# First layer of a two-layer kernel: steps that begin with a quarter of the tokens, a bit-search router, rows moved by indirect DMA

## The chip, the cores and the metric

The kernel runs on one core of a Trainium2 chip. The metric is the device time of one execution in microseconds. The core's engines each run their own instruction stream in order: TensorE (PE; its weight loads are shown as PEld), VectorE (DVE), ScalarE (ACT), GpSimd (POOL) and SyncE (SP), which issues most of the DMAs.

## What is computed

Two layers over one sequence of 2048 tokens of width 128. Each layer computes `x = x + s * silu(f)` from `xn = layernorm(x)`. In the first layer `s` is an attention with relu in place of softmax, 16 heads of width 8, and `f` is a routed transformer block over few tokens. The second layer (causal softmax attention, 16 heads of width 64, and a gated feed-forward) isn't touched by the change.

```python
# first layer, s: relu attention over all 2048 tokens
q, k, v = split((xn @ w_qkv).reshape(B, S, 16, 24))
w = relu(q @ k.T / sqrt(8))
out = (w / (sum(w) + 1e-6)) @ v
s = layernorm(xn + out @ w_out + b_out) * gamma + beta
# first layer, f: the routed block
weights = xn @ router_w + router_b
topv, topi = top_k(weights, 256)
thr = topv[-1]
sel_mask = weights > thr
sel_idx = sort(topi[:255])
x_sel, pos_sel, w_sel = xn[sel_idx], pos[sel_idx], weights[sel_idx]
...   # rmsnorm, 16-head softmax attention with rope, rmsnorm, gelu feed-forward
proc = x2 * w_sel
f = zeros_like(xn).at[sel_idx].set(proc) + xn * (1 - sel_mask)
```

## The kernel before

**Steps.** `relu_attention` runs the first layer as 256 steps. Step n belongs to a query chunk of 512 tokens (n // 64), a group of four heads (n // 16 % 4) and a block of 128 keys (n % 16). `scores(n)` makes four matmuls at once in four row strips of the array (L824), each 32 rows deep, and four relus of 512 columns (L832 on ScalarE, L834 on VectorE). `products(n)` comes two steps later and multiplies the relus by the values (L840). The scores have six PSUM banks, all other work has one bank called `x`.

**High and low parts.** Queries and keys are given to TensorE as a rounded high part and a low rest, so that a group of four heads fills 128 rows: per head 4 combinations of 8 values. For head group 0 a projection makes that layout directly (`project`, L703, L708, L709). For the other groups `spread` (L728 to L738) projects 512 tokens for all heads, makes both parts and writes them by four DMAs of 256 KB into a DRAM tile; `group` (L742) reads one head group of it back, 256 KB, into `kT` or a query tile.

**Before the steps.** `begin` normalises all four blocks of 512 tokens (`normalised`, L774 to L785, then four transposes L101 and a copy L103 into `xnT`), projects the keys of all four blocks for head group 0, the queries of block 0, and the values of all 16 key blocks (`values`, L756, L760). Then step 0 begins.

**Who else works among the steps.** TensorE, ScalarE and VectorE take their instructions in the order of the program. GpSimd and SyncE do not: the framework's planner orders theirs, by what it finds ready. After each step either one piece of `due` is done (a projection with its spread) or the generator `others()` goes on by one turn, that is, to the next `yield`. The generator is the routed block, then the loading of second-layer weights, then the closing of each query chunk (`gated`), which waits until its chunk is `ready`. `work` keeps two running sums, of ScalarE and VectorE microseconds as the author put them down, and `work.lesser` gives each relu to the engine with the lesser sum. These lines set the places:

```python
    due = {1: (all_queries, 0)}
    read = {}
    for i in range(NQ):
        due[4 + 4 * i] = (all_keys, i)
        for g in range(1, G):
            read[8 + 4 * i if g == 1 else 16 * g - 10 + 3 * i] = (g, i)
    for qc in range(1, NQ):
        due[64 * qc - 24] = (all_queries, qc)
```

**The routed block** (`routed_block`). Its set-up (loads, iotas and memsets) precedes its first `yield`, which is taken before `begin`. It makes the router weights of all tokens as a row on every partition (`wrow`, L281, L282) and turns them into columns of 128 (`wcol`, L289, L290). For each of 16 columns it counts on VectorE how many tokens stand ahead of each of the column's 128 tokens (L303, L310, L314): the token's rank, ties by position. From the ranks it makes one-hot matrices (L331) and gathers the selected 256 rows, with weight, index and position, by matmul (L341, sums in L346); a further matmul (L353) takes the threshold. A mask gather by indirect DMA, two normalisations, attention, feed-forward and `proc` (L626) follow. The result is put in place by one-hot matmuls over all tokens (one-hots L642, matmuls L652), added to the unselected rows (L658), and gated (L667 to L674).

In turns: the router rows and columns take steps 0 to 10, the counts 11 to 36, the gather 37 to 46, the block 47 to 127, the placing 128 to 139. From 224 to 255 the generator has nothing to do but wait for the last chunk.

Of the kernel before, what the change touches and what calls it, by code (L numbers as in the profile page):

```python
# [35 lines left out]
NS = 6  # L36
NEG = -1.0e30
# [68 lines left out]
def layer0(ctx, tc, a, small, ident, xin, xn1T, row_load, second):  # L106
# [17 lines left out]
    w_k = keep.tile([P, 4, 4, HD0], F32, name="w_k")  # L124
    w_q = keep.tile([P, 4, 4, HD0], F32, name="w_q")
    for i in range(4):
        for t, dst in ((1, w_k), (0, w_q)):
            nc.gpsimd.tensor_copy(dst[:, :, i, :], w_qkv[:, 0, :, t, :])
# [9 lines left out]
    for n, bit in (("k", 16), ("q", 8)):  # L138
        b = small.tile([P, 1], I32, tag="low_bit")
        nc.vector.tensor_scalar(b, prow, bit, None, ALU.bitwise_and)  # L140
        f = keep.tile([P, 1], F32, name=f"low_{n}")
        nc.vector.tensor_copy(f, b)
        nc.vector.tensor_scalar(f, f, -1.0 / bit, None, ALU.mult)
        lows.append(f)
# [72 lines left out]
def routed_block(  # L217
# [12 lines left out]
    for t, n in enumerate(("wq", "wk", "wv")):  # L230
# [11 lines left out]


    tok = rb.tile([P, 512], F32, name="tok")
    nc.gpsimd.iota(
        tok, pattern=[[1, 512]], base=0, channel_multiplier=0,
        allow_small_or_imprecise_dtypes=True,
    )
    before = rb.tile([P, P], F32, name="before")
    nc.gpsimd.memset(before, 1.0)  # L250
    nc.gpsimd.affine_select(
        out=before, in_=before, pattern=[[-1, P]], compare_op=ALU.is_gt,
        fill=0.0, base=0, channel_multiplier=1,
    )
    last = rb.tile([P, P], F32, name="last")
    nc.gpsimd.memset(last, 1.0)
    nc.gpsimd.affine_select(
        out=last, in_=last, pattern=[[0, P]], compare_op=ALU.is_ge,
        fill=0.0, base=-(P - 1), channel_multiplier=1,
    )  # L260
    nc.gpsimd.iota(
# [5 lines left out]
    qk = rb.tile([P, 2 * H, 32], F32, tag="qk_p4", name="qk")  # L267
    nc.gpsimd.memset(qk, 0.0)
    v = rb.tile([P, 2, H, 32], F32, name="r_v")
# [3 lines left out]
    yield  # L273
# [20 lines left out]


    junk = rb.tile([P, S], BF16, tag="junk_mrows", name="junk")
    cnt = rb.tile([P, 3, NC], F32, name="cnt")
    nc.vector.memset(cnt, 0.0)
    for c in range(NC):
        w = wcol[:, c : c + 1]  # L300
        lo = c * P
        if c:
            nc.vector.tensor_scalar(  # L303
                junk[:, :lo], wrow[:, :lo], w, None, ALU.is_ge, ALU.add,
                accum_out=cnt[:, 0, c : c + 1],
            )
            if c >= NC // 2:
                work.add(d=0.2 + lo / 960)
                yield
        nc.vector.tensor_scalar(  # L310
            junk[:, lo:], wrow[:, lo:], w, None, ALU.is_gt, ALU.add,
            accum_out=cnt[:, 1, c : c + 1],
        )
        nc.vector.scalar_tensor_tensor(  # L314
            junk[:, :P], wrow[:, lo : lo + P], w, before, ALU.is_equal, ALU.mult,
            accum_out=cnt[:, 2, c : c + 1],
        )
        work.add(d=2.9 if c < NC // 2 else 2.7 - lo / 960)
        yield
    rank = rb.tile([P, NC], F32, name="rank")  # L320
    nc.vector.tensor_reduce(rank, cnt.rearrange("p a c -> p c a"), AX.X, ALU.add)
# [3 lines left out]
    made = []  # L325
    for c in range(-2, NC, 2):
        hots = made
        if c + 2 < NC:
            made = [rw.tile([P, KSEL], F32, tag="og", bufs=4, name="hot") for _ in range(2)]
            for i in range(2):  # L330
                nc.vector.tensor_scalar(  # L331
                    made[i], tok[:, :KSEL], rank[:, c + 2 + i : c + 3 + i], None, ALU.is_equal
                )
            work.add(d=0.7)
        if c < 0:
            yield
            continue
        t = bank([P, 2, 131])
        for b in range(2):
            for i in range(2):  # L340
                nc.tensor.matmul(  # L341
                    t[:, b, :], hots[i][:, b * P : (b + 1) * P], xne[:, c + i, 0:131],
                    start=(i == 0), stop=(i == 1),
                )
        if c:
            nc.vector.tensor_tensor(xs, xs, t, ALU.add)  # L346
        else:
            nc.vector.tensor_copy(xs, t)
        work.add(d=0.5)
        yield  # L350
    thr = small.tile([P, 1], F32, tag="thr")
    t = bank([P, 1])
    nc.tensor.matmul(t, last, xs[:, 1, 128:129], start=True, stop=True)  # L353
    nc.vector.tensor_copy(thr, t)
# [278 lines left out]
    at = small.tile([P, 2, NQ], F32, tag="at")  # L633
    for i in range(NQ):
        nc.gpsimd.tensor_scalar(at[:, :, i], xs[:, :, 129], 512.0 * i, None, ALU.subtract)
    for i in range(NQ + 1):
        if i:
            put = place
        if i < NQ:
            place = [rw.tile([P, 512], F32, tag="prT", bufs=4, name=f"place{b}") for b in range(2)]  # L640
            for b in range(2):
                nc.vector.tensor_scalar(place[b], tok, at[:, b, i : i + 1], None, ALU.is_equal)  # L642
            work.add(d=1.0)
            yield
        if not i:
            continue
        cs = slice(4 * i - 4, 4 * i)
        t = bank([P, 4, D])
        for c4 in range(4):
            for b in range(2):  # L650
                n = KB[b]
                nc.tensor.matmul(  # L652
                    t[:, c4, :], put[b][:n, c4 * P : (c4 + 1) * P], proc[:n, b, :],
                    start=(b == 0), stop=(b == 1),
                )
# [21 lines left out]
        yield  # L677


def relu_attention(  # L680
# [19 lines left out]
    def project(dst, w, i, low, tag="x"):  # L700

        t = bank([P, 512], tag)
        nc.tensor.matmul(  # L703
            t, w.rearrange("p b a d -> p (b a d)"), xnT[:, 512 * i : 512 * i + 512],
            start=True, stop=True,
        )
        high = aw.tile([P, 512], F32R, tag="high", name="high")
        nc.scalar.copy(high, t)  # L708
        nc.vector.scalar_tensor_tensor(dst, high, low, t, ALU.mult, ALU.add)  # L709
        work.add(a=0.6, d=0.75)  # L710

    def keys(i):
        project(kT[:, 0, 512 * i : 512 * i + 512], w_k, i, low_k, "s")
# [7 lines left out]
    def queries():  # L721
        project(query_tile(0, 0), w_q, 0, low_q, "s")

    def spread(w, i, order):

# [8 lines left out]
        nc.vector.scalar_tensor_tensor(parts[1], parts[0], -1.0, t, ALU.mult, ALU.add)  # L734
        work.add(a=0.6, d=0.75)
        rows = dram.tile([G, 4, 4, HD0, 512], F32, tag="spread", bufs=8, name="spread")
        for n, x in enumerate(order):
            nc.sync.dma_start(out=rows[:, :, n, :, :], in_=parts[x].bitcast(F32))  # L738
        return rows

    def group(rows, g, dst):
        nc.sync.dma_start(out=dst.bitcast(F32), in_=rows[g].rearrange("j n d q -> (j n d) q"))  # L742

    asked, key_rows = {}, {}

    def all_keys(i):
        key_rows[i] = spread(w_ka, i, (0, 0, 1, 1))

    def all_queries(qc):
        asked[qc] = spread(w_qa, qc, (0, 1, 0, 1))  # L750
# [43 lines left out]

    def begin():
        parts = [normalised(i) for i in range(NQ)]
        next(parts[0])
        for i in range(NQ):
            if i + 1 < NQ:
                next(parts[i + 1])  # L800
# [925 lines left out]
```

## Time and profile before

| | us |
|---|---|
| median of 3 runs | 1487.89 (1487.07 to 1488.57) |
| the profiled execution | 1487.12 |
| its span, first to last instruction | 1485.1 |
| first scores of step 0 | 37.7 |
| first scores of step 12 | 63.1 |
| first scores of step 38 | 115.4 |
| first scores of step 128 | 296.9 |
| end of the 256 steps | about 503 |

In the profile "busy" is the time in which an engine had an instruction at work. Lines such as L824 are lines of the kernel as printed above. A stretch names the busy microseconds of each engine with the number of instructions in brackets, then the mean granted TensorE clock (1.00 is full), the share of the DMA engines that was busy, and GB/s. A row of the timeline has its start, its length, engine, line, operation, output and inputs, shape and count; neighbours of one kind are merged. A float32 matmul shows as two records. SPq marks the issue of a DMA by SyncE, not the transfer.

### The profile page before, as it was taken

To read this page: it belongs to the slowest core of one execution; us is meant where nothing else is said; L and a number is where in the kernel's file an instruction comes from. 1 tells how busy PE (TensorE), PEld (TensorE's weight loads), DVE (VectorE), ACT (ScalarE), POOL (GpSimd) and SP (SyncE) were. 2 spreads that over 40 slices of the span, in tenths; PEclk is the share of its full clock that TensorE was granted. 3 is DMA by queue.
4 is the path that set the end of the run, shared out by engine and by line. 5 is a ranking of instruction groups with operands and counts; after the bars stand their busy time and mean duration, and the time that the engine had idled before them with its cause. 6 is when DMAs were issued, how large, how long until landed. Compare 5 with 4: busy or idle time off the path is not lost.

```text
span 1485.1 us, 27124 instructions
## 1 busy us (share of the span) xinstructions
PE 1431.8 (96%) x10336; PEld 877.3 (59%) x10336; DVE 1079.6 (73%) x1938; ACT 967.2 (65%) x2080; POOL 325.2 (22%) x445
## 2 busy tenths in 40 slices
PE   4999999999999999999999999999999999999997
PEld 2223233332222367777777777777777777777775
DVE  5797878778888667567677667667767766777765
ACT  2787878778878656656556556556656655665663
POOL 1001000050000123322332242242242232252310
PEclk8999999999999999999999999999999999999999
DMA  2621100100200220000010010010001001000000
GB/s 66 186 66 61 32 12 14 49 26 14 60 20 4 79 50 15 15 16 15 21 24 15 15 30 15 15 29 15 15 15 29 15 15 29 15 15 16 15 22 22
DMA packets 28192, 44.70 MB, mean 30 GB/s; under 512 B 5984, under 2 KB 14560, under 8 KB 28064
## 3 DMA queue, kind: packets, MB, share of 16 engines
q1 hardware_dynamic: 27376, 41.94, 11.0%
q8 instruction: 81, 1.33, 0.4%
q0 software_dynamic: 256, 0.79, 0.2%
q14 instruction: 47, 0.39, 0.1%
q10 hardware_dynamic: 432, 0.26, 0.1%
HBM read 14.76 MB, written 10.11 MB: 17 GB/s over the span
## 4 chain that ended last, share of the span: by engine, by line
PE 60%; ACT 2%; DVE 1%; issue 1%; DVEq 0%; ACTq 0%
PE t L1326 18%; PE z L1376 17%; PE t L1556 16%; PE m L1436 2%; PE m L1264 2%; PE m L1229 2%; PE m L1279 2%; PE m L1421 2%; ACT p L1360 1%; ACT pt L1563 1%; PE m L1158 0%; DVE tops L1347 0%; PE m L1176 0%; DVE t L1346 0%; DVE pt L1563 0%
## 5 line engine op out<-in xcount | busy, mean ns | idle before, releaser
L1347 DVE TENSOR_REDUCE tops<-t 128x1 f32<-128x1024 f32 (+4 forms) x320 | 334.6, 1062 | 63.2 <-PE t L1326 56.0
L832 ACT ACTIVATE rt<-t 128x512 f32<-128x512 f32 x620 | 326.3, 625 | 76.1 <-PE t L824 75.0
L1563 ACT COPY pt<-t 128x512 f32<-128x512 f32 (+3 forms) x359 | 163.4, 518 | 266.9 <-PE t L1556 265.8
L1360 ACT ACTIVATE p<-t,tops 128x1024 f32<-128x1024 f32 (+7 forms) x384 | 331.2, 882 | 2.9 <-DVE tops L1347 2.2
L1326 PE MATMUL t<-k,q 128*128 128x512 f32 (+4 forms) x1280 | 316.6, 390 | 7.4 <-ACT p L1360 7.4
L834 DVE TENSOR_SCALAR rt<-t 128x512 f32<-128x512 f32 x404 | 261.2, 684 | 45.4 <-PE t L824 38.6
L840 PE MATMUL t<-rt,va 128*9 128x512 f32 x2048 | 270.3, 601 | 4.2 <-ACT part L856 3.8
L1556 PE MATMUL t<-ident,p 128*128 128x128 f32 x2176 | 270.1, 275 | 3.0 <-ACT x L1250 1.4
L1376 PE MATMUL z<-pt,v 128*64 128x256 f32 (+1 forms) x2304 | 268.3, 374 | 0.5 <-ACT zs L1570 0.5
L1326 PEld LDWEIGHTS t<-k,q 128*128 128x128 f32 x1280 | 218.6, 189 | 79.7 <-issue 36.1
L1556 PEld LDWEIGHTS t<-ident,p 128*128 128x128 f32 x2176 | 244.0, 141 | 25.5 <-ACT pt L1563 2.9
L1376 PEld LDWEIGHTS z<-pt,v 128*64 128x64 f32 x2304 | 151.6, 136 | 86.9 <-issue 21.4
L824 PEld LDWEIGHTS t<-qT,kT 32*128 32x128 f32 x1024 | 64.8, 183 | 189.0 <-ACT rt L832 112.9
L1563 DVE COPY pt<-t 128x512 f32<-128x512 f32 (+3 forms) x289 | 163.5, 605 | 2.6 <-PE z L1376 1.5
L824 PE MATMUL t<-qT,kT 32*128 32x512 f32 x1024 | 157.3, 500 | 4.5 <-DVE rt L834 3.1
L1346 DVE TENSOR_TENSOR t<-t,mask_q 128x128 f32<-128x128 f32 (+1 forms) x192 | 65.0, 339 | 85.8 <-PE t L1326 78.3
L1252 POOL CAST q<-x 64x512 fp32r<-64x512 f32 x60 | 36.8, 613 | 371.7 <-ACT x L1250 338.9
L1360 ACT ACTIVATION_READ_ACCUMULATOR p<-t,tops 128x1 f32 x384 | 84.1, 219 | 0.0
L1426 DVE TENSOR_TENSOR zs<-zs,m 128x512 f32<-128x512 f32 (+1 forms) x49 | 32.7, 676 | 64.3 <-PE m L1421 64.1
L1254 POOL TENSOR_TENSOR k<-x,k 64x512 fp32r<-64x512 f32 x60 | 76.4, 1273 | 4.6
L1254 POOL TENSOR_TENSOR q<-x,q 64x512 fp32r<-64x512 f32 x60 | 76.3, 1272 | 4.6
L840 PEld LDWEIGHTS t<-rt,va 128*9 128x9 f32 x2048 | 30.7, 88 | 69.5 <-issue 61.0
(291 smaller groups left out, 1068.1 us busy)
## 6 DMA issues: line engine op xcount, KB each, us to landing
q<-q SPq DMA_DIRECT2D x64, 256.0 KB
spread<-high SPq DMA_DIRECT2D x16, 256.0 KB
spread<-low SPq DMA_DIRECT2D x16, 256.0 KB
qT<-spread SPq DMA_DIRECT2D x15, 256.0 KB
kT<-spread SPq DMA_DIRECT2D x12, 256.0 KB
xin<-in_x SPq DMA_DIRECT2D x4, 256.0 KB
on<-part SPq DMA_DIRECT2D x64, 16.0 KB
wide<-inverse SPq DMA_DIRECT2D x32, 32.0 KB
```

Of the source, the lines that this page charges most:

```text
L824: nc.tensor.matmul(t, kT[rows, g, kb * P : (kb + 1) * P], qTs[qc, g][rows, :], start=True, stop=True,)
L832: nc.scalar.activation(rt, t, AF.Relu, scale=scale)
L834: nc.vector.tensor_scalar(rt, t, scale, 0.0, ALU.mult, ALU.max)
L840: nc.tensor.matmul(acc[32 * j : 32 * j + HD0 + 1, :], va[:, kb, 4 * g + j, :], r[j], start=(kb == 0), stop=(kb == NC - 1),)
L1254: nc.gpsimd.tensor_tensor(low, x[half(e), :], high, ALU.subtract)
L1326: nc.tensor.matmul(flat[:, at_x : at_x + y - x], q[:, part, c4 * P : (c4 + 1) * P], k[:, x:y], start=(part == 0), stop=(part == 1),)
L1346: nc.vector.tensor_tensor(last, last, mask, ALU.add)
L1347: nc.vector.tensor_reduce(M[pr, c // 4][:, h, c % 4, es], x, axes, ALU.max, negate=True)
L1360: nc.scalar.activation(dst, x, AF.Exp, bias=M[pr, c // 4][:, h, c % 4, e : e + 1], accum_out=Z[pr, c // 4][:, h, c % 4, e : e + 1],)
L1376: nc.tensor.matmul(l1.z[half(e), slot, lo:2, :], V[pr, h][:, kb, half(e)], pts[e][:, kb, lo:2, :], start=(kb == 0), stop=(kb >= n0 - 1), s ...
L1556: nc.tensor.transpose(t[:, k + b, :], x[lo + b], ident)
L1563: copy(dst, t)
```

## The change

It touches the first layer alone.

- `begin` makes only what step 0 to 3 need: block 0's tokens, keys, queries and values, block 1's tokens and the first half of block 2's normalisation. The rest is in `due` at steps 0 to 11, a function for each piece; a piece may return a second half that runs after the next step's scores.
- Head group 0 of blocks 2 and 3 no longer has a projection of its own: it is copied by DMA from the parts that `spread` has made. The DRAM tile holds the two parts as they are (two writes of 256 KB), and reading a group is four DMAs of 64 KB, each to every fourth partition of the destination.
- The router finds the threshold's bits in five rounds: in each, partition p tries one candidate value, counts over the whole row how many weights reach it, and a matmul adds up over the partitions how many candidates are reached by 256 weights. Slots come from prefix sums over the columns and two matmuls. Which token has which slot comes from bf16 one-hots and matmuls of two columns.
- The rows (with weight, index, position) are written to DRAM and the 256 selected are read by two indirect DMAs; the results are written by two indirect DMAs into a DRAM tensor that was filled with zeros, and read back by four DMAs.
- The set-up of the routed block now follows its first `yield`; the generator's first turn among the steps is at step 10. The routed block ends its threshold work three turns earlier than before and its last turn 17 later (steps 44 in place of 47, and 156 in place of 139, counted from the `yield`s).

```diff
-    for i in range(4):
-        for t, dst in ((1, w_k), (0, w_q)):
-            nc.gpsimd.tensor_copy(dst[:, :, i, :], w_qkv[:, 0, :, t, :])
+    for t, dst in ((1, w_k), (0, w_q)):
+        for i in range(4):
+            nc.gpsimd.tensor_copy(dst[:, :, :, i], w_qkv[:, 0, :, t, :])
...
+    yield
+    tok = rb.tile([P, KSEL], BF16, name="tok")
...
+    fields = rb.tile([P, len(SHIFTS)], I32, name="fields")
+    for i, shift in enumerate(SHIFTS):
+        nc.gpsimd.tensor_scalar(
+            fields[:, i : i + 1], number, float(2**shift), None, ALU.mult
+        )
...
+    back = dram.tile([S + 1, D], F32, tag="back", bufs=1, name="back")
+    nothing = rw.tile([P, 4, D], F32, tag="prT", bufs=4, name="nothing")
+    nc.gpsimd.memset(nothing, 0.0)
+    for i in range(NQ):
+        nc.sync.dma_start(
+            out=back[512 * i : 512 * i + 512, :].rearrange("(c p) d -> p c d", p=P), in_=nothing
+        )
...
+    rows = dram.tile([S, 131], F32, tag="rows", bufs=1, name="rows")
+    nc.sync.dma_start(out=rows.rearrange("(c p) d -> p c d", p=P), in_=xne[:, :, 0:131])
...
+    for i in range(len(SHIFTS)):
+        nc.vector.tensor_tensor(tried, bits, fields[:, i : i + 1], ALU.bitwise_xor)
+        nc.vector.tensor_scalar(
+            junk, wrow, tried.bitcast(F32), None, ALU.is_ge, ALU.add, accum_out=cnt
+        )
+        nc.vector.tensor_scalar(enough, cnt, float(KSEL), None, ALU.is_ge)
+        work.add(d=2.9)
+        yield
+        yield
+        t = bank([P, 1])
+        nc.tensor.matmul(
+            t, ones[:, 2 if i == len(SHIFTS) - 1 else 1, :], enough, start=True, stop=True
+        )
+        nc.vector.tensor_scalar(found, t, float(2 ** SHIFTS[i]), None, ALU.mult)
+        nc.vector.tensor_tensor(bits, bits, found, ALU.bitwise_xor)
...
+    for i in range(5):
+        x, y, n = sums[i % 2], sums[1 - i % 2], 1 << i
+        nc.vector.tensor_copy(y[:, :n], x[:, :n])
+        nc.vector.tensor_tensor(y[:, n:], x[:, n:], x[:, : 2 * NC - n], ALU.add)
...
     for c in range(NC):
-        w = wcol[:, c : c + 1]
-        lo = c * P
...
-        nc.vector.tensor_scalar(
-            junk[:, lo:], wrow[:, lo:], w, None, ALU.is_gt, ALU.add,
-            accum_out=cnt[:, 1, c : c + 1],
-        )
...
-                nc.tensor.matmul(
-                    t[:, b, :], hots[i][:, b * P : (b + 1) * P], xne[:, c + i, 0:131],
-                    start=(i == 0), stop=(i == 1),
-                )
...
+        nc.vector.tensor_scalar(hots[:, c, :], tok, slot[:, c : c + 1], None, ALU.is_equal)
+        work.add(d=0.35)
+        if c % 4 == 3:
+            yield
...
+    for b in range(2):
+        t = bank([P, 2])
+        for c in range(NC):
+            nc.tensor.matmul(
+                t, hots[:, c, b * P : (b + 1) * P], place[:, c, :],
+                start=(c == 0), stop=(c == NC - 1),
+            )
...
+        nc.gpsimd.indirect_dma_start(
+            out=xs[:, b, :], out_offset=None, in_=rows[:, :],
+            in_offset=bass.IndirectOffsetOnAxis(ap=token[:, b : b + 1], axis=0),
+        )
+        yield
...
+    for _ in range(5):
+        yield
...
+    for b in range(2):
+        nc.gpsimd.indirect_dma_start(
+            out=back[:, :], out_offset=bass.IndirectOffsetOnAxis(ap=home[:, b : b + 1], axis=0),
+            in_=proc[:, b, :], in_offset=None,
+        )
+    came = []
     for i in range(NQ):
...
+        t = rw.tile([P, 4, D], F32, tag="prT", bufs=4, name="came")
+        nc.sync.dma_start(
+            out=t, in_=back[512 * i : 512 * i + 512, :].rearrange("(c p) d -> p c d", p=P)
+        )
+        came.append(t)
+    for _ in range(12):
+        yield
...
-                nc.tensor.matmul(
-                    t[:, c4, :], put[b][:n, c4 * P : (c4 + 1) * P], proc[:n, b, :],
-                    start=(b == 0), stop=(b == 1),
-                )
...
-        yield
+        for _ in range(4):
+            yield
...
+        def split():
+            nc.vector.scalar_tensor_tensor(parts[1], parts[0], -1.0, t, ALU.mult, ALU.add)
+            rows = dram.tile([2, P, 512], F32, tag="spread", bufs=8, name="spread")
+            return [p.bitcast(F32) for p in parts], rows
...
+    def kept(parts, rows):
+        for n, part in enumerate(parts):
+            nc.sync.dma_start(out=rows[n], in_=part)
+
+    def group(parts, order, g, dst):
+
         for n, x in enumerate(order):
-            nc.sync.dma_start(out=rows[:, :, n, :, :], in_=parts[x].bitcast(F32))
...
+            nc.sync.dma_start(out=dst.bitcast(F32)[n::4, :], in_=parts[x][32 * g : 32 * g + 32, :])
...
     def all_keys(i):
-        key_rows[i] = spread(w_ka, i, (0, 0, 1, 1))
+        split = spread(w_ka, i)
+
+        def later():
+            parts, rows = split()
+            if i >= 2:
+                key_group(parts, i, 0)
+            kept(parts, rows)
+            key_rows[i] = [rows[n] for n in range(2)]
+
+        return later
...
     def begin():
...
+        next(tokens[0])
+        next(tokens[1])
+        next(tokens[0])
+        k = keys(0)
+        next(tokens[1])
+        q = queries()
+        k()
+        next(tokens[2])
+        q()
         values(0)
...
+        work.a, work.d = 0.0, 3.0
...
+    def more(i):
+
+        next(tokens[i])
+        work.add(a=0.6, d=2.0)
+        if i + 1 < NQ:
+            next(tokens[i + 1])
+            work.add(a=0.2, d=1.8)
...
-    due = {1: (all_queries, 0)}
-    read = {}
+
+    due = {
+        0: (more_keys,), 1: (more, 2), 2: (all_keys, 2), 3: (more_values, 1), 4: (more, 3),
+        5: (all_keys, 3), 6: (more_values, 2), 7: (all_keys, 1), 8: (all_queries, 0),
+        9: (more_values, 3), 11: (all_keys, 0),
+    }
+    read = {
+        9: (2, 1), 10: (3, 1), 12: (1, 1), 14: (0, 1),
+    }
     for i in range(NQ):
-        due[4 + 4 * i] = (all_keys, i)
-        for g in range(1, G):
-            read[8 + 4 * i if g == 1 else 16 * g - 10 + 3 * i] = (g, i)
+        for g in range(2, G):
+            read[16 * g - 10 + 3 * i] = (i, g)
...
+        if later:
+            later()
+            later = None
```

## The prediction

> **What bounds the kernel now.** I read the busy times first, then the chain that ended last, then the busy times by stretch, the stretches cut at the starts of the first layer's steps (the groups of four L824 matmuls).
>
> ```profile
> PE 1431.8 (96%) x10336; PEld 877.3 (59%) x10336; DVE 1079.6 (73%) x1938; ACT 967.2 (65%) x2080; POOL 325.2 (22%) x445
> ...
> PE 60%; ACT 2%; DVE 1%; issue 1%; DVEq 0%; ACTq 0%
> ```
>
> TensorE carries 60% of the chain, the others 2% at most: time goes only where TensorE loses work or idle time.
>
> ```profile
> core 0: us, PE busy (x) PEld busy (x) DVE busy (x) ACT busy (x) POOL busy (x), PEclk, DMA share, GB/s
> 0.00:37.73 37.73, 16.32 (x58) 9.52 (x58) 20.75 (x84) 9.14 (x17) 7.09 (x34) 0.86 0.27 65
> 37.73:63.05 25.32, 24.98 (x159) 7.24 (x158) 17.28 (x31) 17.04 (x32) 0.21 (x1) 1.00 0.57 176
> 63.05:77.04 13.99, 13.51 (x92) 3.46 (x89) 13.77 (x29) 13.66 (x29) 0.00 (x0) 1.00 0.78 241
> 77.04:101.35 24.31, 21.98 (x136) 5.56 (x132) 24.13 (x52) 19.97 (x41) 0.00 (x0) 0.86 0.20 61
> 101.35:115.35 14.00, 13.18 (x100) 3.43 (x97) 14.00 (x29) 13.36 (x28) 0.00 (x0) 1.00 0.04 8
> 115.35:139.87 24.52, 24.52 (x192) 11.61 (x189) 16.62 (x42) 15.96 (x32) 0.86 (x4) 1.00 0.17 54
> ```
>
> The rows are the prologue, then steps 0-11, 12-18, 19-29, 30-37 and 38-47. In the prologue TensorE works 16 of 38 us. In 0-11 and 38-47 it is full. In 12-37 VectorE is full (13.8 of 14.0, 24.1 of 24.3, 14.0 of 14.0) with ScalarE close: there the rank counts set the pace. Where nothing is inserted a step lasts 1.41 us (TensorE rows from one step to the next), so 256 steps cost 361 of the 465 us that this layer's steps take. The 982 us after them aren't touched.
>
> **The change part by part**, against the profiled execution (span 1485.1, time 1487.12, which is 0.8 below the median).
>
> *Prologue.* Three of four blocks' normalisation, projection and values leave it. Block 0's first transposes still come at 11.4, its copy to xnT ends at 13.2. Then on TensorE: keys, block 1's transposes, queries, values of block 0.
>
> ```profile
> 17.87 1.91 PE L703 MATMUL t<-xnT,w_q 128*128 128x512 f32 x2
> ...
> 34.10 1.02 PE L703 MATMUL t<-xnT,w_k 128*128 128x512 f32 x2
> ```
>
> At the slow clock: 1.9 + 1.2 + 1.9 + 1.4 = 6.4, so 19.6. On VectorE: block 1's tail (1.9, from 12.0 on), the key combination 0.75, block 2's statistics 1.8, the query combination 0.75 behind ScalarE's copy: about 19.3. Step 0 starts at 19.5: **-18.2**. GpSimd's set-up is longer (3 us more of iotas and memsets, and it is hoisted to the start, as the memset of L425 is, at 9.7, though its place in the program is step 55); in before, two such memsets held VectorE for 1.4 us at 8.6, so I allow 18.5 to 21.5. The four zero loads of 256 KB fall where the SP queue has nothing from 10.9 to 41.8.
>
> Here a rule is weighed. The two L703 rows show one matmul pair at 1.91 and at 1.02, and after 4.6 us of back-to-back work (15.1 to 19.8) it was still slow. The Trainium skill, "TensorE: Matmul & The Clock Gate", section "What's actually happening", says that the array starts at half clock and is released after one busy window of about 3.4 us, windows running freely. By the rule TensorE, dense from 13.2, is fast in step 0 at the latest; by the row steps 0 and 1 still lose about 1.5 us. I take the rule, and keep 1.5 for the range.
>
> *Steps 0-11.* TensorE floor 12 x 1.41 = 16.9. Added: keys of block 1 1.06 (a step with a 512-column pair lasts 2.47), two sets of transposes 0.6 each, five spreads at 1.06, three values at 0.9 (24 records in 2.84), one router row 1.06: 28.3. In steps 1 and 4 the transposes wait for VectorE's normalisation queued behind its own relus (0.8 small operations, 1.1 for the four normalisations, in step 1 also 0.75 and a relu): 2 us each. ScalarE takes the relus meanwhile and covers the 2 us of statistics. 32.3 against 25.3: **+7.0**.
>
> *Steps 12-18.* Three router rows at 1.06, four column turns at 0.59, no spread: 9.9 + 3.2 + 2.4 = 15.4. Then step 16, which reads key group 1 of block 0. Before, its spread stood at step 4; now at step 11, split in step 12, written to DRAM, read back by four strided DMAs.
>
> ```profile
> 49.33 1.18 SPq L738 DMA_DIRECT2D spread<-high  x2
> 50.55 1.78 SPq L738 DMA_DIRECT2D spread<-low  x2
> 55.77 1.28 SPq L742 DMA_DIRECT2D kT<-spread  x3
> ...
> L874 SPq DMA_DIRECT2D wide<-inverse x32: 478/587/599, 341.0 to 522.4; - x32
> ```
>
> From the last write issued (52.3) to the first read 3.4 us for 1 MB; I take 2.3 for half the bytes. A strided read costs SP 0.59 (L874), and `on` could be multiplied 2.0 after the last of them was issued. So: split 2.4 into step 12 (two relus first), writes 1.2, landing 2.3, four reads 2.4, landing 2.0: 10.3 after step 12 starts. Steps 12-15 last 2.47 + 2.0 + 2.47 + 2.0 = 8.9. Wait 1.4 at least. The last row of the first three shows the other danger: groups 1, 2 and 3 were all read at 55.8, though the program asks for 2 and 3 at steps 22 and 38; SP's order is the planner's, by readiness. Ahead of block 0 could stand 18 + 18 + 14 issues of blocks 2, 3, 1 and 10 of the queries: 60 x 0.59 = 35 us from 29 on, plus waits for landings; block 0 then arrives at about 77 against 61: wait 16. Near the low end if urgent reads go first; I take 3. Sum 18.4 against 14.0: **+4.4**.
>
> The Trainium skill, "DMA: Bandwidth & Descriptors", section "Rules for kernel authors", speaks against this part: coalesce, since under 64 KB one pays mostly overhead, and here each 256 KB read becomes four of 64 KB. By its fixed 2 us per DMA ("Anatomy of one DMA"), one after the other, four would take 8 us and step 16 would wait 5 us; by the L861 and L874 rows the latencies overlap and only 0.6 of issue each counts. The row decides.
>
> *Steps 19-29.* Sixteen rank counts leave (about 2.9 of VectorE each, 46 us in all); five full passes come.
>
> ```profile
> L310 DVE TENSOR_SCALAR_CACHE_REDUCE junk<-wrow,wcol 128x2048 bf16<-128x2048 f32 x1 | 2.3, 2347 | 0.0
> L331 DVE TENSOR_SCALAR hot<-tok,rank 128x256 f32<-128x256 f32 x16 | 4.9, 346 | 0.0
> ```
>
> A round is 2.35 + 0.08 and four small operations at 0.16: 3.1 on VectorE in two steps, beside eight relus, of which ScalarE takes 6.5 (0.54 each, 3.5) and VectorE 1.5 (0.65 each, 1.0): 4.1, and 0.1 for the turn through TensorE, whose one-column matmul waits for `enough` with the next step's scores queued behind it. Five rounds 21.0, the first count's step 2.1: 23.1 against 24.3: **-1.2**. The saved VectorE time thus gives little here: the rounds are dense. (Before also lost some 5 us to a half-clock spell at 91.)
>
> *Steps 30-37.* Some 18 small operations, 4.2 for two steps; sixteen one-hots, four a step, 0.35 each by L331, half that if bf16 helps: 1.85 a step (1.55 to 1.95), 7.4; two steps of 16 bf16 matmuls of two columns, between 0.06 and 0.14 each (a float load, L1556, is 0.14): 2.8 each. 17.2 against 14.0: **+3.2**.
>
> *Steps 38-47.* The gather on TensorE goes.
>
> ```profile
> 127.04 1.16 PE L341 MATMUL x<-xne,hot 128*128 128x131 f32 x8
> ...
> 301.97 2.05 PE L652 MATMUL x<-proc,place 128*128 128x128 f32 x16
> ```
>
> Now five bare steps 7.1, the query spread 2.5, then what stood at 47-50 (6.4): 16.1 against 24.5: **-8.4**. The indirect reads land 4.1 us after issue (as `mcols`), and seven steps lie between: nothing, and 4 us if that cover failed.
>
> *The scatter.* Four times 2.05 (L652), which TensorE did between bare steps: **-8.2**; the STTs stay. Two indirect writes (2.2 issue, 4.1 landing) and four loads (5 us) take about 12; twelve empty turns give 17. Without that cover VectorE would hold the relus behind `came`. On SP the loads wait for the writes with the next group's `sums` and `on` copies behind them; `part` has two buffers and is wanted again 16 steps later. The tail ends 17 turns later, but steps from 224 on were bare, so it stays inside.
>
> Sum: -18.2 + 7.0 + 4.4 - 1.2 + 3.2 - 8.4 - 8.2 = -21.4. Median 1487.9 - 21.4 = **1466.5**.
>
> **The rivals.**
> - *The queue is late* (0.17): 16 at step 16 in place of 3, so 1479.5. For it: three reads at once at 55.8. Against: the program's order still ranks them when several are ready.
> - *VectorE is freed* (0.16): with 31 us of counting gone, TensorE runs at its floor: 19-29 in 17, 30-37 in 13.8, 1457. For it: VectorE was full in 12-37. Against: a relu every 0.3 us fills both engines already.
> - *Slower* (0.08): SP again, one mechanism: if besides those 60 the 2 MB of zeros and rows stand ahead of block 0 (1 MB of 512-byte rows took 5.5 us at the start, 178 GB/s), block 0 comes 11.5 us later still and step 16 waits 27.5: 1491. It decides from a wait of 24.4 on, key reads after about 85.
> - *No net gain* (0.04): a wait between 21.5 and 27.5. That the change doesn't do what it says is excluded for the moved matmuls, whose rows go; the hoisting could only undo it through SP.
>
> **How the numbers follow.** The likeliest (0.55) is 1466.5. Unknowns: step 0 +-1.5, clock 1.5, step 16 from 1.4 to 16, one-hots and small matmuls +-3, rounds -6. The range 1455 to 1482 reaches both nearer rivals and leaves out the slow cases and the sum of all luck. Over 0.2% (3 us, about what a measurement here can tell from no change): faster 0.88, within 0.04, slower 0.08.
>
> **What would show it.** First L824 group near 19.5; step 12 near 52; a gap before the 17th group and what SP was issuing then; steps of about 2.1 during the five counts; no L341 and L652 rows; bare steps after the proc product. Wrong would be: a step 16 later than 70, rounds above 5 us, or VectorE waiting on `xs` or `came`.

## The result and the profile after

| | us |
|---|---|
| before, median of 4 runs | 1487.48 (1487.02 to 1488.57) |
| after, median of 4 runs | 1465.71 (1463.30 to 1467.68) |
| after / before | 0.9852 (95% interval 0.9840 to 0.9865) |
| the profiled execution after | 1466.11 |
| its span | 1464.4 |

The forecast of 1466.5 was met to 0.8 us. The stretches below are cut at the same steps as those of before (prologue, steps 0-11, 12-18, 19-29, 30-37, 38-47), with a last row for steps 48 to 255 up to the end of the last products; the columns are the same (PE, PEld, DVE, ACT, POOL, clock, DMA share, GB/s).

```profile
0.00:19.23 19.23, 6.78 (x20) 4.03 (x20) 13.83 (x54) 4.62 (x9) 9.51 (x46) 1.00 0.69 182
19.23:55.58 36.35, 31.05 (x174) 10.40 (x174) 20.17 (x50) 21.89 (x43) 0.00 (x0) 0.91 0.32 101
55.58:72.33 16.75, 15.53 (x107) 4.74 (x106) 10.60 (x19) 9.92 (x18) 0.00 (x0) 1.00 0.34 104
72.33:92.67 20.34, 18.37 (x144) 5.64 (x144) 18.34 (x39) 16.60 (x33) 0.21 (x1) 1.00 0.62 116
92.67:108.27 15.60, 14.30 (x139) 4.98 (x136) 12.66 (x49) 14.08 (x29) 0.94 (x1) 1.00 0.16 40
108.27:124.09 15.82, 15.82 (x126) 3.90 (x124) 13.10 (x28) 12.42 (x28) 3.28 (x5) 1.00 0.27 80
124.09:479.80 355.71, 348.46 (x2800) 100.58 (x2800) 293.23 (x563) 289.31 (x564) 38.55 (x68) 1.00 0.10 26
```

Row by row against before: -18.5, +11.0, +2.8, -4.0, +1.6, -8.7, -7.3, in all -23.1; the span is 20.7 shorter. The other 2.4 lie behind the layer's steps. From the start of step 255 to the end, before takes 984.2 us and after 986.6; all kernels of this study, with the same work there, take 984.0 to 988.2, so 2.4 lies within their spread. In steps 0-11 TensorE now stands still for 5.3 of 36.35 us and its granted clock is 0.91, where before it was busy for 24.98 of 25.32 at full clock. In 12-37 VectorE is no longer full (10.6 of 16.75, 18.3 of 20.3, 12.7 of 15.6).

The clock column counts nothing ahead of the first clock record (18.0 in after, 20.0 in before). Up to there the matmuls took about twice as long, in both kernels; the same pair of after, ahead of that record and behind it:

```profile
13.12 2.05 PE L786 MATMUL t<-xnT,w_k 128*128 128x512 f32 x2 [0.77 <-ACT xnT L104]
...
19.67 1.13 PE L786 MATMUL t<-xnT,w_k 128*128 128x512 f32 x2
```

Where TensorE waits in steps 0 to 12, by the timeline of after (start, length, engine, line; in brackets the idle time ahead of it and who ended it):

```profile
24.50 1.15 PE L102 MATMUL t<-ident,xne 128*128 128x128 f32 x4 [2.62 <-DVE xne L895]
...
34.86 1.25 PE L102 MATMUL t<-ident,xne 128*128 128x128 f32 x4 [1.65 <-DVE xne L895]
...
47.09 1.12 PE L810 MATMUL t<-xnT,w_qa 128*128 128x512 f32 x2 [1.02 <-DVE low L819]
...
58.16 1.12 PE L326 MATMUL x<-xnT,rwb 128*128 128x512 f32 x2 [1.10 <-DVE low L819]
```

The first two are the transposes of steps 1 and 4 that wait for the normalisation. The last two are matmuls that want the one PSUM bank `x`, still held by the spread of the step before: its second half, `low`, was put off behind the next step's relus.

The rows of the new router and gather in steps 19 to 47, from the groups of that stretch:

```profile
L363 DVE TENSOR_SCALAR_CACHE_REDUCE junk<-wrow,tried 128x2048 bf16<-128x2048 f32 x5 | 11.7, 2347 | 0.2
...
L413 DVE TENSOR_SCALAR hots<-tok,slots 128x256 bf16<-128x256 bf16 x16 | 3.4, 280 | 0.0
...
L371 PE MATMUL x<-enough,ones 128*128 128x1 f32 x10 | 1.9, 255 | 2.3 <-DVE enough L366 2.2
...
L422 PE MATMUL x<-place,hots 128*128 128x2 bf16 x32 | 1.1, 164 | 0.0
```

Five passes of 2.35 replace the counts. TensorE waits for `enough` 2.2 us in all. The 32 two-column matmuls cost 1.1 together.

### The profile page after: what moved, and what is told of

Its sections match the earlier page's. It is cut to its first block, busy times and chain, and to the rows that moved or that the text cites. A ratio compares the mean times of both kernels' runs of the same rounds, so it can differ in the third digit from the quotient of the medians.

```text
span 1464.4 us, 27046 instructions
## 1 busy us (share of the span) xinstructions
PE 1412.4 (96%) x10250; PEld 863.5 (59%) x10250; DVE 1057.6 (72%) x1905; ACT 955.1 (65%) x2055; POOL 329.8 (23%) x457
## 3 DMA queue, kind: packets, MB, share of 16 engines
q0 software_dynamic: 384, 1.05, 0.3%
## 4 chain that ended last, share of the span: by engine, by line
PE 61%; ACT 2%; DVE 1%; issue 1%; DVEq 0%; ACTq 0%
PE t L1458 18%; PE z L1508 17%; PE t L1688 16%; PE m L1568 2%; PE m L1396 2%; PE m L1361 2%; PE m L1411 2%; PE m L1553 2%; ACT p L1492 1%; ACT pt L1695 1%; PE m L1290 0%; DVE tops L1479 0%; PE m L1308 0%; DVE t L1478 0%; DVE pt L1695 0%
## 5 line engine op out<-in xcount | busy, mean ns | idle before, releaser
L1479 DVE TENSOR_REDUCE tops<-t 128x1 f32<-128x1024 f32 (+4 forms) x320 | 334.6, 1062 | 63.1 <-PE t L1458 56.0
L956 ACT ACTIVATE rt<-t 128x512 f32<-128x512 f32 x597 | 315.4, 605 | 64.7 <-PE t L948 63.3
L958 DVE TENSOR_SCALAR rt<-t 128x512 f32<-128x512 f32 x427 | 275.7, 684 | 70.0 <-PE t L948 64.9
L948 PE MATMUL t<-qT,kT 32*128 32x512 f32 x1024 | 152.6, 499 | 2.7 <-ACT rt L956 1.9
L1558 DVE TENSOR_TENSOR zs<-zs,m 128x512 f32<-128x512 f32 (+1 forms) x49 | 32.7, 675 | 65.8 <-PE m L1553 65.7
L1384 POOL CAST k<-x 64x512 fp32r<-64x512 f32 x60 | 36.6, 609 | 158.6 <-ACT x L1382 156.8
```

The lines of the kernel that those rows point to most:

```text
L948: nc.tensor.matmul(t, kT[rows, g, kb * P : (kb + 1) * P], qTs[qc, g][rows, :], start=True, stop=True,)
L956: nc.scalar.activation(rt, t, AF.Relu, scale=scale)
L958: nc.vector.tensor_scalar(rt, t, scale, 0.0, ALU.mult, ALU.max)
L1384: nc.gpsimd.tensor_copy(high, x[half(e), :])
L1479: nc.vector.tensor_reduce(M[pr, c // 4][:, h, c % 4, es], x, axes, ALU.max, negate=True)
```

## The experiments

The theory after this comparison: the two parts add, the beginning being worth -18.5 + 11.0 + 2.8 = -4.7 and the router with its transfers the rest; what of the beginning's 18.5 is lost again goes to the waits just shown. The rivals: the beginning is worth nothing, since its idle time only moves; and the waits have no price, since the layer gives back what is won early. Ratios below are to the kernel before, run beside each on the same chip.

**Each part alone.** `e1_first_only`: after, with the router, gather and scatter of before.

```diff
-    yield
...
-    tok = rb.tile([P, KSEL], BF16, name="tok")
...
+    tok = rb.tile([P, 512], F32, name="tok")
...
-    rows = dram.tile([S, 131], F32, tag="rows", bufs=1, name="rows")
...
+    rank = rb.tile([P, NC], F32, name="rank")
...
```

(The whole of `routed_block` is exchanged for that of before, so its set-up stands ahead of its first `yield` again.)

> Changed kernel with the router, the gather and the scatter of the kernel before put back: only the earlier beginning of the steps is left of the change. Theory (the parts add): prologue -18.5, steps 0 to 11 +11.0, steps 12 to 18 +2.8 as in the trace of the changed kernel, nothing after step 18: -4.7, so about 1482.8. By the terms of the prediction it would be -18.2 + 7.0 + 4.4 = -6.8, 1480.7. Rival (the parts depend on each other: the counts of ranks fill VectorE, so the beginning's deferred work comes on top of them): no gain or a loss, 1487 or more.

Measured: 1487.77, ratio 0.9997 (0.9988 to 1.0006): nothing. The rival is right for the beginning alone.

`e2_router_only`: the reverse.

```diff
+SHIFTS = (24, 17, 10, 3, 0)
...
-    tok = rb.tile([P, 512], F32, name="tok")
+    tok = rb.tile([P, KSEL], BF16, name="tok")
...
```

> Kernel before with the router by bits, the rows moved by indirect DMA and the scatter through DRAM of the changed kernel: only that part of the change. Theory (the parts add): steps 19 to 29 -4.0, 30 to 37 +1.6, 38 to 47 -8.7, the scatter -7.3: -18.4, about 1469. By the terms of the prediction -1.2 + 3.2 - 8.4 - 8.2 = -14.6, 1472.9. Rival (router and beginning help each other): less than -12, 1475 or more.

Measured: 1472.30, ratio 0.9885 (0.9870 to 0.9900): 17 us, between the theory's 18.4 and the 14.6 of the prediction's terms. The rival, less than 12, falls. The stretches of the beginning alone, cut at the starts of steps 0, 19, 48 and 255:

```profile
0.00:19.67 19.67, 6.75 (x20) 3.98 (x21) 13.22 (x54) 4.71 (x9) 7.06 (x34) 1.00 0.48 124
19.67:72.49 52.82, 46.43 (x281) 15.20 (x282) 30.77 (x69) 31.70 (x61) 0.00 (x0) 0.94 0.34 103
72.49:133.49 61.00, 56.75 (x375) 16.59 (x374) 57.61 (x124) 51.02 (x102) 0.21 (x1) 0.94 0.16 45
133.49:501.84 368.35, 361.36 (x2884) 113.56 (x2883) 295.74 (x578) 292.75 (x574) 39.82 (x73) 1.00 0.09 23
```

The same of the router alone:

```profile
0.00:37.78 37.78, 16.54 (x59) 9.65 (x60) 20.28 (x84) 9.14 (x17) 9.51 (x46) 0.95 0.36 92
37.78:78.18 40.40, 38.87 (x253) 11.52 (x252) 29.64 (x54) 29.08 (x55) 0.21 (x1) 1.00 0.71 197
78.18:128.69 50.51, 48.74 (x403) 14.12 (x402) 42.61 (x114) 41.69 (x85) 5.00 (x9) 1.00 0.31 98
128.69:484.32 355.63, 347.79 (x2770) 100.17 (x2766) 291.38 (x553) 287.16 (x560) 37.77 (x64) 0.99 0.10 27
```

Before and after can be added up from the rows shown, but for steps 48 to 254. For before:

```profile
139.87:500.92 361.05, 354.84 (x2842) 107.58 (x2842) 295.50 (x569) 289.81 (x570) 39.28 (x69) 1.00 0.10 26
```

For after these steps last 353.7, of which TensorE is busy for 346.5. Take a stretch's length less TensorE's busy time, and add up:

| up to step 255 | length | PE busy | not busy: prologue, 0-18, 19-47, 48-254 |
|---|---|---|---|
| before | 500.9 | 469.3 | 31.6 = 21.4 + 0.8 + 3.2 + 6.2 |
| beginning alone | 501.8 | 471.3 | 30.6 = 12.9 + 6.4 + 4.3 + 7.0 |
| router alone | 484.3 | 451.9 | 32.4 = 21.2 + 1.5 + 1.8 + 7.8 |
| after | 477.8 | 448.3 | 29.5 = 12.5 + 6.5 + 3.3 + 7.3 |

Of the prologue's 18.5 only 9 are idle time of TensorE. The other 9.5 are busy time (16.3 against 6.8). About 3 of them, by an estimate from the clock records, are less time at half clock: up to 20.0 and from 23.4 to 33.6 before, up to 18.0 after. Two of four key matmuls are gone. The rest, one key matmul, two sets of transposes and three of values, is now done in the steps. Of the 9 us of idle time 7 come back: 5.7 in steps 0 to 18, the others behind them. The clock in steps 0 to 18 is also at half for two windows of 3.4 us (0.94); before had none there. So the whole change leaves TensorE 2 us less idle; what it wins is TensorE's busy time, 21 us, of which 17.4 come with the router alone.

A lead at step 19 (4.6 for the beginning alone) is not yet a gain. The router is then six turns behind where it stands before, and they are paid after step 48 (368.35 against 361.05), where five turns of the gather now fall.

**Is it TensorE's work?** `e8_placed` and `e9_gathered` put back the scatter and the gather alone.

```diff
-    back = dram.tile([S + 1, D], F32, tag="back", bufs=1, name="back")
...
-    for b in range(2):
-        nc.gpsimd.indirect_dma_start(
-            out=back[:, :], out_offset=bass.IndirectOffsetOnAxis(ap=home[:, b : b + 1], axis=0),
...
+                nc.vector.tensor_scalar(place[b], line, at[:, b, i : i + 1], None, ALU.is_equal)
...
+                    t[:, c4, :], put[b][:n, c4 * P : (c4 + 1) * P], proc[:n, b, :],
```

```diff
-    rows = dram.tile([S, 131], F32, tag="rows", bufs=1, name="rows")
...
-        nc.gpsimd.indirect_dma_start(
-            out=xs[:, b, :], out_offset=None, in_=rows[:, :],
...
+                    made[i], tok, slot[:, c + 2 + i : c + 3 + i], None, ALU.is_equal
...
+                    t[:, b, :], hots[i][:, b * P : (b + 1) * P], xne[:, c + i, 0:131],
```

> Changed kernel with the scatter of the kernel before (one-hot places and matmuls; no rows written to DRAM and read back). Theory (TensorE's work sets the time of these steps): its four times 2.05 come back whole, +8.2, less at most 0.5 for the zeros that are no longer made at the start: about 1473.5. Rival (the layer has idle time that would hide them, as it swallowed the earlier beginning): +3 or less, 1469 or less.

> Changed kernel, rows gathered on TensorE by one-hot matmuls as before, with the new slots in place of the old ranks. Theory: the eight turns of 1.16 come back (9.3), two steps of two-column matmuls (2.20 and 1.90 against bare 1.41: 1.3) and four turns of one-hots go: about +8, 1473.7. Rival (hidden in idle time): +3 or less.

Measured: 1475.76, ratio 0.9923 (0.9906 to 0.9940), and 1471.88, ratio 0.9893 (0.9877 to 0.9910): 10.5 and 6.1 above after by the ratios, each with some 3 of uncertainty (12.9 and 8.5 by the second measurement of after, 0.9836, below). Both come back, neither is hidden. The scatter's row, from the groups of the stretch 275 to 345 of e8:

```profile
L735 PE MATMUL x<-proc,place 128*128 128x128 f32 (+1 forms) x64 | 8.2, 280 | 0.0
```

The scatter's 8.2 are there to the digit; steps 128 to 159 last 58.6 for 48.8, so the waits around it cost another 1.5. The gather's turns take 1.16 each, as before (five of them 5.8 in the stretch 108 to 132 of e9).

**Do the waits have a price?** `e3_turn_later` sets the transposes of blocks 2 and 3 two steps behind the normalisation.

```diff
     def normalised(i):
...
+        if i >= 2:
+            yield
         transposed(
...
-        0: (more_keys,), 1: (more, 2), 2: (all_keys, 2), 3: (more_values, 1), 4: (more, 3),
...
-        9: (more_values, 3), 11: (all_keys, 0),
+        0: (more, 2), 1: (more_keys,), 2: (turn, 2), 3: (all_keys, 2), 4: (more, 3),
...
+        9: (all_keys, 1), 10: (all_queries, 0), 11: (all_keys, 0), 12: (more_values, 3),
...
```

> Changed kernel, with the transposes of token blocks 2 and 3 issued two steps after VectorE's normalisation instead of directly behind it. Theory: the two waits of TensorE (2.62 and 1.65) go, and with them the two windows of half clock that follow, about 1.2 each: steps 0 to 11 last some 30 to 31 us instead of 36.35, time 1460 (1459 to 1462). Rival A: only the waits go, the half-clock windows have another cause: 1462. Rival B: the wait comes back at the scores, whose banks wait for the relus behind the normalisation on VectorE: 1465 to 1466.

`e4_split_first` and `e11_spread_first` set the deferred halves, all or those of the spreads alone, ahead of the next scores; `e12_both` joins the latter with e3. (In e4 the condition is `if later` alone.)

```diff
+        if later and due[n - 1][0] in (all_keys, all_queries):
+            later()
+            later = None
         if n < n_steps:
             held.append((n, scores(n)))
         if later:
```

> Changed kernel, with the deferred second half of a spread issued ahead of the next step's scores and relus instead of behind them. Theory: the bank of the spread comes free before the next step needs it, the two waits for VectorE's split at steps 8 and 12 (1.02 and 1.10) go: 2 us less, 1463.5. Rival: VectorE then waits for ScalarE's copy ahead of its relus in each of the nine steps with a deferred half, some 0.4 us each: 0 to +2, 1466 to 1468.

> Changed kernel, with only the spreads' deferred half (not that of the keys and queries of group 0) ahead of the next step's scores. Theory: the 2 us that the bank held are won in steps 8 to 16 as when all deferred halves went first, without the 1.8 that the keys' half cost there in steps 0 to 3, and they stay won: 1463.5. Rival (a wait taken out early is given back later in the layer, as with the later transposes): 1465 to 1466.

> Changed kernel, with the transposes two steps after the normalisation and the spreads' deferred half first. Theory (TensorE's waits are lost one by one: 4 us at step 12 with the later transposes alone, eaten later in part by the bank that the query spread of step 104 held for 2.1, which is now released): 2 less from the banks, 2 to 4 from the transposes, 1459.5 to 1461.5. Rival (layer one gives back what is won early): 1464 to 1466.

| | median us | ratio | its profiled run: us, step 0 at, step 12 at, step 16 at |
|---|---|---|---|
| after | 1465.71 | 0.9840 to 0.9865 | 1466.11, 19.2, 55.6, 65.9 |
| e3_turn_later | 1465.37 | 0.9822 to 0.9852 | 1466.73, 18.7, 51.7, 61.8 |
| e4_split_first | 1466.47 | 0.9839 to 0.9869 | 1466.22, 19.2, 56.7, 65.7 |
| e11_spread_first | 1465.71 | 0.9834 to 0.9866 | 1463.54, 17.7, 54.2, 63.1 |
| e12_both | 1466.28 | 0.9841 to 0.9874 | 1460.58, 18.0, 48.4, 59.9 |

In the medians nothing is left: the times that the theory gave (1459.5 to 1463.5) are all missed, and the rivals are right about the time.

In the steps the theory holds only in part. By step 12 e3 stands 3.9 us ahead of after and e12 7.2, but most of that is not won. Their step 0 came 0.5 and 1.3 earlier. And with two pieces more in `due` they put off a set of values and a router row past step 12 (1.16 and 1.12 in after). At step 48 all have issued the same matmuls. Counted from step 0, e3 is there at 103.4 and e12 at 102.3, after at 104.9. In e3 the waits shrink as foreseen: TensorE stands still for 3.6 us of steps 0 to 18, for 6.5 in after. The half-clock time does not shrink: it is 6.8 us in both, so here e3's rival A was right. In e4 and e11 the places in `due` stay. There the bank wins 2.3 in steps 8 to 15, and steps 0 to 3 lose 1.8 and 0.9, as their clock is at half for 6.8 us in place of 3.4.

Of e3's lead 2.1 us go at step 105: the routed attention's turn, 1.07 us long, waits for the `x` bank, which the query spread of step 104 holds. In after this turn came ahead of the spread.

```profile
242.22 1.07 PE L655 MATMUL x<-prT,r_v 128*32 128x256 f32 x16 [1.06 <-DVE low L819]
```

**The same kernels again.** `e0_after_again` is after, unchanged; `e13_both_again` is e12.

> The changed kernel again, beside the next. Expected 1465.7, within 1.5; the start of step 16 within 0.5 of 65.9. If the free-running clock windows decide about the small differences between the variants, its runs spread over some 4 us and the half-clock windows of its profile stand elsewhere than at 24.8, 35.1, 164.8, 526.6 and 1444.8.

> The kernel with later transposes and the spreads' half first again: its profiled run took 1460.6, with two half-clock windows ahead of the last, its other runs 1465.6 to 1468.8. Theory A (its own steps are 5 us shorter, and half-clock windows that fall otherwise in most runs take it back): the new profiled run has step 19 near 66.8 whatever the clock; where its time is over 1463, the trace shows three or more half-clock windows more. Theory B (the first run was chance): step 19 near 70.

Measured, five runs each: after 1463.78, ratio 0.9836 (0.9823 to 0.9850); both 1464.86, ratio 0.9839 (0.9826 to 0.9853). No difference. e0 missed both of its own figures (1463.78 for 1465.7 within 1.5, step 16 at 64.3 for 65.9 within 0.5); its half-clock windows stood elsewhere, as its expectation had it. Two stretches of after in its first profiled run (steps 4 to 7, steps 64 to 95), then the same in its second:

```profile
31.73:44.59 12.86, 11.21 (x66) 3.60 (x66) 7.01 (x17) 6.95 (x13) 0.00 (x0) 0.87 0.40 124
...
155.38:222.59 67.21, 66.07 (x538) 24.01 (x535) 53.42 (x81) 53.59 (x110) 0.00 (x0) 0.97 0.05 13
```

```profile
31.61:43.22 11.61, 9.96 (x65) 3.36 (x64) 7.02 (x17) 6.86 (x13) 0.00 (x0) 1.00 0.44 137
...
154.05:219.78 65.73, 64.59 (x539) 23.70 (x535) 53.34 (x81) 53.60 (x110) 0.00 (x0) 1.00 0.05 13
```

VectorE and ScalarE do the same to 0.1 us; only the clock differs, and takes 1.25 and 1.48 of the 3.1 by which these two executions of one kernel lie apart (1466.11 and 1462.97). Half-clock windows stand at 24.5, 492.1 and 526.2 in the second, at 24.8, 35.1, 164.8, 526.6 and 1444.8 in the first (the last of each run left out). So a difference of 2 us can't be told in four or five runs. That doesn't hide the 4 to 6 us that the theory gave for e12: measured side by side, the two ratios leave room for less than 3.

For e12, theory A asked for step 19 near 66.8 and for three or more further half-clock windows, theory B for step 19 near 70. The windows are there: two in place of one in steps 0 to 11, one at 63.7, and two in place of one in the 70 us behind the layer's steps. But step 19 came at 70.7, as B had it (52.0 after step 0, where the first run took 48.8 and the two of after 53.1 and 51.5). The first run was in part chance. Once the early waits are gone, step 16 waits for its keys, 1.94 us in the first run; in the second run its first scores, with the idle time ahead of them:

```profile
62.22 0.51 PE L954 MATMUL t<-qT,kT 32*128 32x512 f32 x4 [2.62 <-DMA kT<-spread]
```

and what SP was issuing then:

```profile
51.53 0.32 SPq L827 DMA_DIRECT2D spread<-low  x1
51.94 3.40 SPq L832 DMA_DIRECT2D qT<-spread  x4
55.38 7.84 SPq L832 DMA_DIRECT2D kT<-spread  x12
```

The keys of block 0 are written at 51.5. The four reads of the query group, which step 16 needs too, take 3.4 us of the queue. By the landings in the trace it is the eighth key read (issued at 59.84, landed at 62.08) that lets step 16 begin, so four other key reads stood ahead of block 0's. That is the late queue of the prediction's rival, at a small size.

**The way to step 16, and the rule on coalescing.** `e6_key0_late` sets the spread of block 0's keys two steps later; `e7_key0_late_one_read` also takes the DRAM layout of before.

```diff
-        9: (more_values, 3), 11: (all_keys, 0),
+        9: (more_values, 3), 13: (all_keys, 0),
```

In e7 also:

```diff
+        for n, x in enumerate(order):
+            nc.sync.dma_start(out=rows[:, n, :], in_=parts[x])
...
+            out=dst.bitcast(F32), in_=rows[32 * g : 32 * g + 32].rearrange("p n q -> (p n) q")
```

> Changed kernel, the spread of the keys of block 0 two steps later (13 for 11), so that the way of its group 1 through DRAM to step 16 is no longer covered. Theory (10.3 us from the start of the step that splits it, here step 14): steps 14 and 15 last 4.5, so TensorE waits 5.8 ahead of step 16, and loses up to 1.7 more in a half-clock window behind that: step 16 starts at 71.5 to 73.5 for 65.9; time 1471 to 1473, less what of it is given back later. Rival (SP issues reads of other groups ahead of it, which the planner already hoists): 72 or later by far, wait 10 and more, 1476.

> As the one before, with the DRAM layout of the kernel before: each spread written by four DMAs of 256 KB, each group read back by one DMA of 256 KB in place of four of 64 KB. By the coalescing rule (each DMA pays its fixed 2 us) three times 2 us go from the way to step 16: wait about 0, 5 us less than the kernel before this in the list. By the row (only SP's issue of 0.6 each counts, latencies overlap): 1.8 less for the reads, 1.6 more for the two further writes and their bytes: within 1.5 of it.

Measured: 1468.14, ratio 0.9867 (0.9852 to 0.9882), and 1469.70, ratio 0.9873 (0.9858 to 0.9888). In e6 step 14 starts at 60.2 and step 16 at 67.8: 7.6 in place of the theory's 10.3, with a wait of 1.96 where 5.8 was expected, so its times for step 16 and for the whole are missed, and the rival's too. In e7 it is 60.1 and 69.1: 9.0, with a wait of 3.42; within 1.5 of e6, as the reading by the row had it, and not 5 less. The issues on SP, first e6, then e7:

```profile
60.99 0.33 SPq L827 DMA_DIRECT2D spread<-high  x1
61.36 0.45 SPq L832 DMA_DIRECT2D kT<-spread  x1
62.68 0.32 SPq L827 DMA_DIRECT2D spread<-low  x1
63.05 7.46 SPq L832 DMA_DIRECT2D kT<-spread  x12
```

```profile
62.49 0.80 SPq L827 DMA_DIRECT2D spread<-low  x2
64.20 0.32 SPq L830 DMA_DIRECT2D qT<-spread  x1
66.33 1.27 SPq L830 DMA_DIRECT2D kT<-spread  x3
```

The landings in the traces give the way step by step. In e6 `low` is written at 62.68 and lands at 64.81. The two reads of the high half go out before that (63.62 and 64.19), those of the low half at 64.88 and 65.46, and the last lands at 67.65. In e7 the last of four writes is issued at 62.86 and lands at 66.24; the one read goes out at 66.33 and lands at 69.03. So e7 changes two things, and the 1.4 us lie in the first: its writes are four in place of two and land later. From the last write's landing to the last read's it is 2.84 with four reads and 2.79 with one.

The rule (the Trainium skill, "DMA: Bandwidth & Descriptors", section "Rules for kernel authors") speaks for the one read, and the estimate made from it was 5 us; in these two traces the one read is worth 0.05. That estimate took 2 us for each read, one after the other. The page gives this figure for DMAs that GpSimd issues. SyncE's took about as long here from issue to landing (2.13 for `low` in e6), but they overlap. The whole times of the two can't be told apart.

## Why the prediction came out right

The total was right to 0.8 us, its terms less so: errors of +4.0, -1.6, -2.8, -1.6 and +0.9 in the stretches, and 2.4 lost behind the layer, nearly cancel. That the direction and most of the size came out is the router's part, where the mechanism was right; that the total came within 0.8 is luck.

- *Prologue, -18.2 (-18.5).* Right in size; the clock rule held, step 0 ran at full clock (0.51 for its scores, the clock record from 18.0 on). What was missing is what the 18 us consist of. The table above shows that 9 of them were idle time, of which 7 come back.
- *Steps 0-11, +7.0 (+11.0).* The two waits for the normalisation were foreseen at 2 and 2 and came at 2.62 and 1.65. Missing was what is beside them: two windows at half clock (the products in steps 2 and 5 took 1.9 for 1.05) and the `x` bank (1.02 in step 8). The sum had neither.
- *Steps 12-18, +4.4 (+2.8).* The wait of 3 at step 16 came to 0.2 (step 15 took 2.19 for 2.00), but not because the way was shorter. From the start of step 12 to the landing of the last read it took 10.25 (55.58 to 65.83), the 10.3 of the sum; in the second run 9.7. Its parts were other ones: `low`, written at 58.13, landed only at 62.83, and two reads came behind it, not four. What had grown is the cover, steps 12 to 15, to 10.3 for 8.9, by 1.1 of waiting for the `x` bank that the sum didn't have. One miss hid the other. Without the bank's wait step 16 did wait, 1.94 in e12; where `low` landed 2.1 after its issue, the way took 7.6 (e6). SP did put the urgent reads first; e13 shows that it need not.
- *Steps 19-29 and 30-37, -1.2 and +3.2 (-4.0 and +1.6).* Half of the fifth round falls into the second row, so they are read together: 4.4 less than forecast. A round takes two steps of 3.5 to 4.3, 3.9 in the mean, where 4.2 was taken throughout; one-hots take 0.28 for 0.35, and the two steps of two-column matmuls 2.20 and 1.90 for 2.8. That makes about 4.
- *Steps 38-47 and the scatter, -8.4 and -8.2 (-8.7 and -7.3).* Right; e8 and e9 show that this work was on the path. The covers hold (the indirect reads landed 2.6 to 2.8 us after issue, where 4.1 was taken): in after's trace VectorE has no idle time that ends with a landing of `came` or of the gathered rows.
- *By parts.* The terms say -6.8 for the beginning and -14.6 for the router. Alone they gave -0.4 (-1.8 to +0.9) and -17.1 (-19.3 to -14.9). After beside the router alone, the beginning is worth 4.9 by the first comparison (0.9852 to 0.9885) and 7.3 by the second (0.9836), each with some 3 of uncertainty, so near the -6.8, but only with the new router. Why it is worth nothing with the old one stays open. By the table it frees 1.0 us of idle time there and 2.9 with the new router, but TensorE's busy time for the same instructions moves by +2.0 and -3.6, and the clock alone shifts single executions by 3; no run here takes these apart.
- *The rival "VectorE is freed"* was half right: VectorE did come free (18.3 of 20.3 in steps 19 to 29), but the steps did not fall to TensorE's floor.

## What to carry to other kernels

Split a stretch into TensorE's work, its idle time and its half-clock time before pricing an earlier start: work that is moved out of a prologue is not saved, and of the idle time 7 of 9 us came back in the steps. Compare leads only where both kernels have issued the same work: those of e1, e3 and e12 were in good part work put off. Work taken off the engine that bounds the kernel is the safe part of such a change: put back, 8.2 and 8 us of it cost 10.5 and 6.1, each with some 3 of uncertainty. A wait removed is worth what is late next: here the `x` bank, then the order of SP's reads.

## What was not expected of the hardware

- **Little idle time halves the clock.** After 1.65 us of idle time ahead of L102 at 34.86, TensorE's clock was at half from 35.1 to 38.5; in the second run of the same kernel the same 1.65, at 34.75, was followed by full clock. Cut into windows of 3.4 us in step with the recorded changes, 36 of the 37 windows of all traces here with 1.85 us or more of idle time were followed by one at half clock, about a third of the 30 with 1.6 to 1.85, and about 15 of nearly 100 with 0.9 to 1.6. Idle time alone doesn't decide: in e3 0.86 us in the window from 20.3 on was followed by two windows at half clock. The Trainium skill, "TensorE: Matmul & The Clock Gate", section "What's actually happening", has free-running windows of this length, and half clock after at least one idle window; here half a window of idle time was enough.
- **A matmul of two columns is cheap but not free:** 164 ns for 128x2 in bf16 (L422) beside 255 for one column of f32 (L371).
- **A strided 64 KB read takes SP 0.45 to 0.6 us to issue, a plain 256 KB write 0.33** (e6), a plain 256 KB read 0.32 to 0.43 (e7). So four reads cost SP more than one, and still gave the keys as soon.
- **A DMA's last share can land far behind the others while instructions are loaded.** The write of `low` at 58.13 raised its semaphore 16 times, 15 times by 60.13 and the last time at 62.83. In between, after's DMA record has one packet of the instruction queue (16 KB, 60.39 to 61.35). Over the first 480 us of the 14 traces, 125 of 720 DMAs with such a packet in flight had a last share more than 1 us late, and 2 of 1537 without one. No run here takes the packets away, so the cause is likely, not shown.
